# Token tiles of 32 frames from each of four batches, reads by row groups, and projections of scaled samples by weights that hold the DCT

## The chip, the cores and the metric

The kernel runs on one core of a Trainium2 chip. TensorE (PE) multiplies matrices from SBUF into PSUM, VectorE (DVE), ScalarE (ACT) and GpSimd (POOL) work on elements, SyncE (SP) issues most transfers. Each engine works through its own queue in order. The metric is the device time of one execution in microseconds: the median of three runs is 1425.93 (1425.9 to 1426.23).

## The reference, cut to what matters

64 signals of 80000 samples are cut into 157 frames of 512 samples each. Then, per signal:

```
h = frames @ D.T                                  # orthonormal DCT, 512 x 512
x = layernorm(h)
k, q = exp(i*pi*tanh(x @ Wk)), exp(i*pi*tanh(x @ Wq))   # 4 sets of 8 planes
v = x @ Wv + bv
for each set s: total += weights[s] * Re( sum over planes( cumsum(k*v) * conj(q) ) )
pos = the same with phases of the position instead of k and q
gate = sigmoid(x @ Wg + bg)
total = gate * total + (1 - gate) * sigmoid(pos_weight) * pos
h = h + x + (total / norm) @ Wo + bo              # norm = sqrt(8 * (t + 1))
x2 = layernorm(h)
scores = softmax(mean over frames(x2) @ Wg2 + bg2); e = argmax
out = h + scores[e] * (x2 @ We[e] + be[e])        # one of 16 experts per signal
```

The cumulative sum with conjugate phases is a causal attention with linear scores: (k . q) masked by j <= t, times v. All is float32.

## The kernel before, in words

The 64 signals are worked in 16 groups of four batches. A group has five tiles of 128 tokens: tile m < 4 holds the first 128 frames of batch m, and the tile `GB` (the tail) holds the last 32 frames of all four batches side by side. Samples arrive in five transfers a group (`load_frame`), already turned so that samples lie on partitions, are folded twice for the symmetries of the DCT (`fold_once`, `fold_twice`), and `embed` makes h of a tile in a PSUM pair: two matmuls of 128 columns for the even coefficients and two of 129 for cosines and sines of the odd ones, which `embed_statistics` puts together on DVE after a copy by ACT. (The first two groups use a direct table for the odd ones, L215.)

`embed_x` normalises the tile (ACT), `turn` transposes it by four TensorE transposes (L174) and a copy (L180), so that xT has features on partitions; `embed_res` keeps h + x. From xT come the phases (`project`, L519), the values (`value`, `value_product`) and the gate (`gate_product`). Values, gate and output projection use a scheme of seven half-size products for eight (`product`, L314 and L573; `token_sums`, `gather`, L317 put operands and results together), the tail tile is multiplied directly (L193).

`scores` makes the masked attention weights of a batch; `read` multiplies the values of a batch by them in full 128-row matmuls of 314 columns (157 for the content, 157 for the positions, L614) and DVE mixes the two by the gate (L604, L605). The 32-row tails are read by `read_tails` (L628), in which the four batches use four row groups of the array, into four PSUM banks; `add_tails` adds them on POOL. `output_product` adds the products into the residuals `res`, partly through u by POOL (L645). Then follow the second statistics (L161 to L168), `normal2` (ACT, L684), `turn_x2`, the routing (`route` to `pick`), an indirect fetch of the chosen expert's 1 MB per batch (`fetch`, L741), and `expert`: one matrix per batch for the tiles 0 to 3 (L193), and for the tail four matrices in four column groups of 32 (L800).

The order of the work is written out by hand: each function issues into the engines' queues in program order, and semaphores hold an instruction until its operands are ready. In group g, `project_and_values(g)` first turns x2 of group g-1, `gate(g)` follows, `experts_and_embedding(g)` runs the experts of g-1 and embeds g+1, and `attention(g)` reads and projects. PSUM is three pairs of banks in rotation (`psum`) and two single banks (`bank`). The products of the output go in the order

```
    PRODUCTS = (1, 2, 6, 5, 7, 3, 4)
```

with the second statistics of tiles 0 and 1 after product 3 and of tiles 2 and 3 after product 4. Product 1 writes r11, 2 r11, 6 r12 through u, 5 r12 and r22, 7 r21 and r22 through u, 3 r12, 4 r21 (r1 are tiles 0 and 1, r2 tiles 2 and 3, the second index the half of the columns).

Of the kernel before, what the change touches and what calls it, by code (L numbers as in the profile page):

```python
# [28 lines left out]
TL = LP - P  # L29
LT = L - P  # L30
NM = GB + 1
# [8 lines left out]
ORDER = [GB, *range(GB)]  # L40
# [3 lines left out]
def audio_tower(ctx: ExitStack, tc: tile.TileContext, a, out):  # L44

# [22 lines left out]
    small = pool("small", 6)  # L68
# [15 lines left out]
    S = [{} for _ in range(NG)]  # L84


    def load_frame(g, m):
        if g < NG:
            ft = p1.tile([P, C, P], F32, tag="frame", name="frame", bufs=NM)
            nc.sync.dma_start(out=ft, in_=a["frames"][g, m])  # L90
            S[g]["frame", m] = ft

    def fold_once(g, m):

        if g < NG:
            ft = S[g]["frame", m]
            even = p2.tile([P, 2, P], F32, tag="even", name="even")
            nc.vector.tensor_tensor(even, ft[:, :2, :], ft[:, 2:, :], ALU.add)  # L98
            nc.gpsimd.tensor_tensor(ft[:, :2, :], ft[:, :2, :], ft[:, 2:, :], ALU.subtract)
            S[g]["even", m] = even  # L100

    def fold_twice(g, m):

        if g < NG:
            ft, even = S[g]["frame", m], S[g].pop(("even", m))
            nc.vector.tensor_tensor(ft[:, 2, :], even[:, 0, :], even[:, 1, :], ALU.add)
            nc.vector.tensor_tensor(ft[:, 3, :], even[:, 0, :], even[:, 1, :], ALU.subtract)
            for n in range(2 if g > 1 else 0):
                to, by = ft[:, n, :], ft[:, 1 - n, :]
                nc.vector.scalar_tensor_tensor(to, by, lift[:, n : n + 1], to, ALU.mult, ALU.add)  # L110


    load_frame(0, 0)
    dct_e = load("dct_e", [P, 2, P])
    dct_o = p1.tile([P, 2, 2 * P], F32, tag="sum0", name="dct_o")
    nc.sync.dma_start(out=dct_o, in_=a["dct_o"])
    load_frame(0, 1)
    load_frame(0, 2)
    wv = load("wv", [P, C, D])
    load_frame(0, 3)  # L120
    load_frame(0, 4)
    lift = load("lift", [P, 2])
    trig_o = load("trig_o", [P, 2, P + 1])
    bv = load("bv", [P, D], a["bv"].partition_broadcast(P))
# [5 lines left out]
    setsel = load("setsel", [2 * F, SETS])  # L130
    hbg = load("hbg", [P, C], a["bg"])
    bo = load("bo", [P, D], a["bo"].partition_broadcast(P))
    wkq = load("wkq", [P, C, 2 * F])
    bkq = load("bkq", [P, 1])
    hmask = load("hmask", [P, L])
    hmask_t = load("hmask_t", [P, LT])
    wg = load("wg", [P, C, D])
    wo = load("wo", [P, C, D])
    rwg = load("rwg", [P, C, TL])
    rbg = load("rbg", [P, GB, E], a["rbg"].partition_broadcast(P))  # L140
    revexp = load("revexp", [P, GB, E])
    rowbase = load("rowbase", [P, 1])

    ident = const.tile([P, P], F32, name="ident", tag="ident")
    make_identity(nc, ident)
    power = const.tile([P, 1], F32, name="power", tag="power")
# [4 lines left out]
    def warm(n):  # L151

        ps = bank()
        for _ in range(n):
            nc.tensor.matmul(ps[:, :P], ident, ident, start=True, stop=True)

# [14 lines left out]
    def transposed(x):  # L171
        tr = bank()
        for c in range(C):
            nc.tensor.transpose(tr[:, c * P : (c + 1) * P], x[:, c * P : (c + 1) * P], ident)  # L174
        return tr

    def place(xT, m, tr, apart=None, copy=nc.scalar.copy):

        if m < GB:
            copy(xT[:, :, m, :P], tr.rearrange("p (c t) -> p c t", c=C))  # L180
            return
        copy(xT[:, :, :, P:], tr.rearrange("p (c b t) -> p c b t", c=C, b=GB))  # L182
        if apart is not None:
            nc.scalar.copy(apart, tr.rearrange("p (c t) -> p c t", c=C))

    def by_tail(t):

        return t.rearrange("p (b t) -> p b t", t=TL)[:, :, :LT]

    def by_tokens(ps, lhs, w):  # L190

        for c in range(C):
            nc.tensor.matmul(ps, lhs(c), w[:, c, :], start=(c == 0), stop=(c == C - 1))  # L193
        return ps


    def embed(g, m):

        s = S[g]
        if m == 0:  # L200
            s["xT"] = p1.tile([P, C, GB, LP], F32, tag="xT", name="xT", bufs=2)
            s["xT_t"] = p1.tile([P, C, P], F32, tag="xT_t", name="xT_t")
            s["res"] = []
            s["res2"] = []
        h = psum()
        h, odd = h[:, 0, :], h[:, 1, :].rearrange("p (n j) -> p n j", n=2)
        ft = s.pop(("frame", m))
        by_r = h.rearrange("p (j r) -> p r j", r=4)
        for i in range(2):
            nc.tensor.matmul(by_r[:, 2 * i, :], ft[:, 2 + i, :], dct_e[:, i, :], start=True, stop=True)  # L210
        for i in range(2):
            if g > 1:
                nc.tensor.matmul(odd[:, i, : P + 1], ft[:, i, :], trig_o[:, i, :], start=True, stop=True)  # L213
            else:
                nc.tensor.matmul(by_r[:, 1::2, :], ft[:, i, :], dct_o[:, i, :], start=(i == 0), stop=(i == 1))  # L215
        s["h", m] = h, odd

    def embed_statistics(g, m):
        s = S[g]
        h, odd = s.pop(("h", m))  # L220
        by_r = h.rearrange("p (j r) -> p r j", r=4)
        if g > 1:
# [825 lines left out]
    for m in order:  # L1048
        bias(g, m)
# [100 lines left out]
```

## Time and profile before

| what | value |
|---|---|
| median of three runs | 1425.93 us |
| the profiled execution | 1428.35 us, its span 1426.6 us |
| TensorE busy | 1414.3 us, 99% of the span, 7346 instructions |
| DVE, POOL, ACT busy | 995.0, 686.0, 493.8 us (70, 48, 35%) |
| granted TensorE clock | 0.999 |
| moved by DMA | 135.54 MB, 95 GB/s in the mean |

The span runs from the first to the last instruction of the profiled execution; its own time is 1.75 us longer. Busy time counts modelled ends of matmuls, which overlap, so for a matmul's price the start of one row of a timeline is subtracted from that of the next. A float32 matmul shows as two instructions and a transpose as one.

### The profile page before, as it was taken

What the parts mean: (1) busy time and instruction counts of PE and PEld (TensorE: products, weight loads), DVE (VectorE), ACT (ScalarE), POOL (GpSimd) and SP (SyncE); (2) the same over time, 40 slices, a digit from 0 to 9 for tenths busy, and PEclk for the clock granted to TensorE, in tenths of its full rate; (3) what the DMA queues carried; (4) which work ended last, traced back from release to release, by engine and by line L of the source; (5) the groups of instructions that cost most, each with busy time, mean ns of one, the idle gap of its engine ahead of it and who ended that gap; (6) DMA issues with size and microseconds to landing.
All of it is one profiled execution on the core that took longest, in us unless ns stands there. A gap on an engine that the chain in (4) does not pass through costs nothing.

```text
span 1426.6 us, 20573 instructions
## 1 busy us (share of the span) xinstructions
PE 1414.3 (99%) x7346; PEld 976.1 (68%) x7346; DVE 995.0 (70%) x2307; ACT 493.8 (35%) x851; POOL 686.0 (48%) x1042
## 2 busy tenths in 40 slices
PE   8999999999999999999999999999999999999998
PEld 5776676766767667676776767667676676766763
DVE  5677667676776777776777767766767677677674
ACT  4533244422434324343233442324433244422420
POOL 4454555345454453544536544455444555445432
PEclk9999999999999999999999999999999999999999
DMA  6104132051420504214042240423304142040405
GB/s 202 38 1 170 59 132 98 1 192 37 156 74 3 212 15 155 75 39 177 14 163 66 76 147 6 163 66 124 105 1 178 50 155 74 1 177 15 155 8 221
DMA packets 43157, 135.54 MB, mean 95 GB/s; under 512 B 8032, under 2 KB 8688, under 8 KB 34480
## 3 DMA queue, kind: packets, MB, share of 16 engines
q0 software_dynamic: 15616, 88.09, 16.2%
q1 hardware_dynamic: 27208, 45.90, 9.9%
q8 instruction: 59, 0.97, 0.3%
q14 instruction: 42, 0.34, 0.1%
q10 hardware_dynamic: 232, 0.24, 0.1%
HBM read 113.62 MB, written 20.58 MB: 94 GB/s over the span
## 4 chain that ended last, share of the span: by engine, by line
PE 94%; DVE 2%; DMA 2%; POOL 1%; issue 1%; another core or an unknown queue 0%; ACT 0%; SPq 0%; POOLq 0%; DVEq 0%
PE mm L314 26%; PE mm L573 15%; PE tr L193 13%; PE mm L614 10%; PE mm L193 8%; PE tr L174 5%; PE mm L800 4%; PE mm L519 2%; PE mm L210 2%; PE mm L213 2%; PE tr L700 1%; PE mm L628 1%; PE tr L590 1%; PE mm L555 1%; DMA frame<-in_frames 1%
## 5 line engine op out<-in xcount | busy, mean ns | idle before, releaser
L193 PE MATMUL tr<-we,x2T 128*128 128x512 f32 x448 | 201.4, 592 | 0.0
L165 POOL TENSOR_SCALAR rstd<-mv 128x1 f32<-128x1 f32 x160 | 39.5, 247 | 317.7 <-DVE mv L163 310.0
L614 PE MATMUL mm<-att,v 128*128 128x314 f32 x512 | 139.7, 431 | 0.0
L193 PEld LDWEIGHTS tr<-we,x2T 128*128 128x128 f32 x448 | 81.7, 190 | 82.5 <-issue 80.4
L317 DVE TENSOR_TENSOR v<-mm,v 128x512 f32<-128x512 f32 x105 | 72.3, 688 | 75.6 <-PE tr L174 50.6
L614 PEld LDWEIGHTS mm<-att,v 128*128 128x128 f32 x512 | 94.5, 189 | 38.3 <-issue 3.8
L583 ACT ACTIVATE gT<-gT,hbg 128x314 f32<-128x314 f32 x120 | 60.3, 551 | 172.4 <-DVE gT L317 166.2
L236 ACT ACTIVATE x<-mm,shift,rstd 128x512 f32<-128x512 f32 x80 | 62.2, 777 | 144.5 <-POOL shift L168 144.5
L166 POOL TENSOR_TENSOR rstd<-rstd,power 128x1 f32<-128x1 f32 x160 | 103.3, 645 | 13.3
L317 DVE TENSOR_TENSOR gT<-mm,gT 128x628 f32<-128x628 f32 x105 | 85.0, 810 | 31.3 <-PE mm L573 27.0
L174 PEld LDWEIGHTS tr<-ident,x 128*128 128x128 f32 x576 | 67.3, 141 | 51.8 <-issue 16.4
L645 POOL TENSOR_TENSOR res<-res,u 128x512 f32<-128x512 f32 x48 | 60.1, 1265 | 73.6 <-DVE u L317 73.6
L741 POOL DMA_INDIRECT we<-in_we,rows x62 | 61.6, 994 | 57.0 <-PE mm L193 40.4
L314 PE MATMUL mm<-t_o,sum 128*128 128x256 f32 x384 | 88.1, 379 | 0.0
L174 PE MATMUL tr<-ident,x 128*128 128x128 f32 x576 | 85.9, 276 | 1.2 <-DVE x2T L182 0.8
L314 PE MATMUL mm<-t_v,sum 128*128 128x256 f32 x360 | 86.7, 384 | 0.0
L317 DVE TENSOR_TENSOR res<-mm,res 128x512 f32<-128x512 f32 x96 | 64.5, 685 | 29.6 <-PE mm L314 19.0
L314 PEld LDWEIGHTS mm<-t_o,sum 128*128 128x128 f32 x384 | 73.0, 190 | 16.7 <-issue 7.7
L778 POOL DMA_INDIRECT be<-in_be,expi x75 | 71.3, 951 | 22.8 <-issue 18.6
L257 POOL TENSOR_TENSOR res<-res,bo 128x512 f32<-128x512 f32 x64 | 80.3, 1282 | 0.0
L314 PEld LDWEIGHTS mm<-t_v,sum 128*128 128x128 f32 x360 | 64.8, 190 | 10.7 <-DVE even L98 3.5
L379 POOL TENSOR_TENSOR v<-v,bv 128x1024 f32<-128x1024 f32 x30 | 70.7, 2358 | 0.0
(198 smaller groups left out, 3004.0 us busy)
## 6 DMA issues: line engine op xcount, KB each, us to landing
frame<-in_frames SPq DMA_DIRECT2D x80, 256.0 KB
out<-be SPq DMA_DIRECT2D x60, 256.0 KB
out<-be SPq DMA_DIRECT2D x60, 32.0 KB
out<-be SPq DMA_DIRECT2D x60, 26.0 KB
be<-in_be,expi POOLq DMA_INDIRECT x75
wv<-in_wv SPq DMA_DIRECT2D x1, 1024.0 KB
wg<-in_wg SPq DMA_DIRECT2D x1, 1024.0 KB
wo<-in_wo SPq DMA_DIRECT2D x1, 1024.0 KB
```

Of the source, the lines that this page charges most:

```text
L166: nc.gpsimd.tensor_tensor(rstd, rstd, power, ALU.pow)
L174: nc.tensor.transpose(tr[:, c * P : (c + 1) * P], x[:, c * P : (c + 1) * P], ident)
L193: nc.tensor.matmul(ps, lhs(c), w[:, c, :], start=(c == 0), stop=(c == C - 1))
L236: nc.scalar.activation(x, h, AF.Identity, bias=shift, scale=rstd)
L257: nc.gpsimd.tensor_tensor(r, r, bo, ALU.add)
L314: nc.tensor.matmul(ps[:, b, :], lhs[:, c, b, :P], w[:, c, :], start=(c == 0), stop=(c == 1))
L317: add = lambda to, x, y: nc.vector.tensor_tensor(to, x, y, ALU.add)
L379: nc.gpsimd.tensor_tensor(v, v, bv.unsqueeze(1).to_broadcast([P, 2, D]), ALU.add)
L573: nc.tensor.matmul(ps[:, o, : 2 * L], w[:, c, o * P : (o + 1) * P], rhs[:, c], start=(c == 0), stop=(c == 1))
L614: nc.tensor.matmul(ps[:, c, : 2 * L], s["v", i][:, cols], att[:, i], start=True, stop=True)
L741: nc.gpsimd.indirect_dma_start(out=w, out_offset=None, in_=a["we"], in_offset=bass.IndirectOffsetOnAxis(ap=s["rows"][:, b : b + 1], axis=0),)
L778: nc.gpsimd.indirect_dma_start(out=be, out_offset=None, in_=a["be"], in_offset=bass.IndirectOffsetOnAxis(ap=s["expi"][:, m : m + 1], axis=0),)
```

## The change

All five tiles of a group now have one form: tile n holds frames 32n to 32n+31 of each of the four batches, a quadrant of 32 rows per batch (`NM` = 5, tile 4 is called `TAIL`). In storage the tiles lie in the order `SLOT` (0, 1, 4, 2, 3), so that two and a half tiles make a half of 320 tokens; samples come in two transfers of halves into the buffer `xT` itself.

- **Weights with the DCT.** Wv, Wk, Wq and Wg are multiplied once, at the start, by the DCT, after their mean over the features is taken off (`through_dct`). Values, phases and gate are then computed from the folded samples, each scaled by its token's rstd. `spread` makes the scaling: rstd of a tile, broadcast, is transposed by one TensorE transpose and DVE multiplies the samples by it in place. `embed` still makes h for the residual and the statistics; `embed_x`, `turn` and their copies go.
- **Reads by quadrants.** `scores` computes, per tile and batch, 32 keys by the queries that can see them (160, 128, 96, 96 and 32 columns), four column groups side by side. `read` works a block of 128 features at a time: for each tile, four matmuls of 32 rows, one per batch, accumulate into four banks over the five tiles. `read_tails`, `add_tails` and the separate tail buffers go.
- **Experts.** Every tile holds all four batches, so every expert tile uses the four matrices in four column groups. One fetch of biases serves all tiles. The output is written in place of the residual, by four transfers a tile and eight for the last.
- **Order.** The products of values and gate go 1, 2, 6, 7, 5, 3, 4, those of the output 1, 2, 4, 6, 7, 5, 3, the output's tail comes before product 7, and the four second statistics follow the last product. The last group's weights are fetched in two parts and its experts go chunk by chunk over all tiles.
- The start is written anew for the weights; x2T has a buffer of its own; residual pairs are five instead of four.

The core of the diff (most removed lines are left out):

```diff
+Q = P // GB
+NM = LP // Q
+TAIL = NM - 1
+SLOT = [0, 1, 3, 4, 2]
+HT = P // 2
+HN = HT + 2 * P
...
+SEES = [(0, LP), (Q, LP), (2 * Q, LP), (2 * Q, LP), (2 * Q, 3 * Q)]
+START = [sum(hi - lo for lo, hi in SEES[:n]) for n in range(NM)]
+NS = sum(hi - lo for lo, hi in SEES)
...
+    def half(x, m):
+        return x[:, :, HN * m : HN * (m + 1)]
+    def tile_of(x, n):
+        return x[..., P * SLOT[n] : P * (SLOT[n] + 1)]
+    def load_half(g, m):
         if g < NG:
+            if m == 0:
+                S[g]["xT"] = p1.tile([P, C, 2 * HN], F32, tag="xT", name="xT", bufs=2)
+            nc.sync.dma_start(out=half(S[g]["xT"], m), in_=a["frames"][g, m])
...
+    def through_dct(raw, to, n):
+        ps = psum()[:, 0, :n]
+        for c in range(C):
+            nc.tensor.matmul(ps, mean, raw[:, c], start=(c == 0), stop=(c == C - 1))
+        sub(raw, raw, ps.unsqueeze(1).to_broadcast([P, C, n]))
+        yield
+        for k, parts in enumerate((((0, 1), (1, 3)), ((2, 1), (3, 3)), ((4, 0),), ((5, 2),))):
+            if k % 2 == 0:
+                ps = psum()
+            for i, (table, r) in enumerate(parts):
+                nc.tensor.matmul(
+                    ps[:, k % 2, :n], tables[:, table], raw[:, r], start=(i == 0), stop=(i == len(parts) - 1)
+                )
+            if k % 2:
+                nc.scalar.copy(to[:, k - 1 : k + 1], ps[:, :, :n])
+                yield
...
+        sines = p2.tile([P, P + 1], F32, tag="sines", name="sines")
+        nc.scalar.copy(sines, odd[:, 1, : P + 1])
+        add(by_r[:, 1, :], odd[:, 0, :P], sines[:, :P])
+        sub(by_r[:, 3, :], odd[:, 0, 1 : P + 1], sines[:, 1 : P + 1])
         rstd, shift = statistics(h)
         rstd1 = small.tile([P, 1], F32, tag="rstd1", name="rstd1")
         nc.gpsimd.tensor_scalar(rstd1, rstd, 1.0, None, ALU.add)
...
+    def embed_res(g, n):
+        s = S[g]
+        h, shift, rstd1 = s.pop(("st", n))
+        if n == TAIL:
             r = p1.tile([P, D], F32, tag="res_t", name="res_t", bufs=2)
         else:
+            if n % 2 == 0:
+                s["res2"].append(p1.tile([P, 2, D], F32, tag="res", name="res", bufs=5))
+            r = s["res2"][-1][:, n % 2, :]
         nc.scalar.activation(r, h, AF.Identity, bias=shift, scale=rstd1)
...
+    def spread(g, n):
+        s = S[g]
+        tr = bank()[:, :P]
+        nc.tensor.transpose(tr, s["rstd", n].to_broadcast([P, P]), ident)
+        x = tile_of(s["xT"], n)
+        nc.vector.tensor_tensor(x, x, tr.unsqueeze(1).to_broadcast([P, C, P]), ALU.mult)
...
+    def alike(first, second):
+        n = 2 * P
+        yield first[:, :, :n], second[:, :, -n:]
+        if first.shape[2] > n:
+            yield first[:, :, n:], second[:, :, :-n]
+    def token_sums(g, x, tail=True):
+        S[g]["blocks"] = blocks = halves(x)
+        n = HN if tail else 2 * P
+        (a11, a12), (a21, a22) = [[y[:, :, :n] for y in blocks[0]], [y[:, :, -n:] for y in blocks[1]]]
+        S[g]["sums"] = made = [
+            p1.tile([P, 2, HN], F32, tag=f"sum{i}", name="sum")[:, :, :n] for i in range(4)
+        ]
+        for (to, x), (_, y) in zip(alike(made[0], a21), alike(made[0], a22)):
+            add(to, x, y)
+        yield
+        sub(made[1], made[0], a11)
+        yield
+        for (to, y), (x, _) in zip(alike(made[2], a21), alike(a11, a21)):
+            sub(to, x, y)
+        yield
+        sub(made[3], a12, made[1])
...
+    def gather(i, ps, c):
         (c11, c12), (c21, c22) = c
         if i == 1:
+            nc.scalar.copy(c12, ps)
         elif i == 2:
+            add(c11, ps, c12)
+        elif i == 7:
+            for (x, to), (y, _) in zip(alike(ps, c21), alike(c12, c21)):
+                add(to, x, y)
+        elif i == 5:
+            add(c12, ps, c12)
+            for (x, to), (_, y) in zip(alike(ps, c22), alike(ps, c21)):
+                add(to, x, y)
+        elif i == 4:
             add(c21, ps, c21)
+        else:
             add(c12, ps, c12)
...
+    def scores(g):
         ps = bank()
+        for n in range(NM):
+            lo, hi = SEES[n]
             for i in range(GB):
+                to = ps[Q * i : Q * (i + 1), START[n] : START[n] + hi - lo]
+                nc.tensor.matmul(to, kf[:, SLOT[n], i], qf[:, lo // Q : hi // Q, i], start=True, stop=True)
+        nc.vector.tensor_tensor(att[:, 0], ps[:, :NS], hmask, ALU.mult)
+        nc.vector.tensor_tensor(att[:, 1], att[:, 0], share, ALU.add)
...
+    def read(g, c):
+        s = S[g]
+        if c % 2 == 0:
+            parts = [psum(), psum()]
+        else:
+            parts = [psum(), bank().unsqueeze(1), bank().unsqueeze(1)]
+        banks = [ps[:, b, : 2 * LP] for ps in parts for b in range(ps.shape[1])]
+        for n in range(NM):
+            for i in range(GB):
+                q = slice(Q * i, Q * (i + 1))
+                lo, hi = SEES[n]
+                to = banks[i].rearrange("p (s t) -> p s t", s=2)[:, :, lo:hi]
+                by = att[q, :, START[n] : START[n] + hi - lo]
+                nc.tensor.matmul(
+                    to, s["v", n][q, c * P : (c + 1) * P], by, start=(n == 0), stop=(n == TAIL)
+                )
+        i = 0
+        for ps in parts:
+            of = slice(i, i + ps.shape[1])
+            i = of.stop
+            r = ps[:, :, : 2 * LP].rearrange("p b (s n t) -> p b s n t", s=2, n=NM)
+            th = s["gT"][:, c].rearrange("p (n b t) -> p b n t", n=NM, b=GB)[:, of]
+            for n, op in enumerate((ALU.mult, ALU.add)):
+                nc.vector.tensor_tensor(th, r[:, :, n], th, op)
...
+    def fetch(g, rooms=(), parts=1):
+        s = S[g]
+        ws = [
+            rooms[b] if b < len(rooms) else p1.tile([P, C * D], F32, tag="we", name="we", bufs=GB) for b in range(GB)
+        ]
+        n = C * D // parts
+        of = a["we"].rearrange("r (k n) -> (r k) n", k=parts)
+        for k in range(parts):
+            rows = t("rows", [P, GB], I32)
+            base = rowbase[:, parts + k - 1 : parts + k]
+            nc.vector.tensor_scalar(rows, s["rev"], float(-P * parts), base, ALU.mult, ALU.add)
+            for b in range(GB):
+                nc.gpsimd.indirect_dma_start(
+                    out=ws[b][:, n * k : n * (k + 1)],
+                    out_offset=None,
+                    in_=of,
+                    in_offset=bass.IndirectOffsetOnAxis(ap=rows[:, b : b + 1], axis=0),
+                )
+        s["ws"] = [w.rearrange("p (c o) -> p c o", c=C) for w in ws]
...
+    def add_bias(g, n):
+        s = S[g]
+        nc.vector.scalar_tensor_tensor(s["res"][n], s["be"], s["gate"], s["res"][n], ALU.mult, ALU.add)
+    def expert_chunk(g, n, c, ps):
+        s = S[g]
+        for i in range(GB):
+            nc.tensor.matmul(
+                ps[Q * i : Q * (i + 1), :],
+                s["x2T"][:, c, i, Q * n : Q * (n + 1)],
+                s["ws"][i][:, c, :],
+                start=(c == 0),
+                stop=(c == C - 1),
+            )
+    def expert_out(g, n, ps):
+        s = S[g]
+        o = s["res"][n]
+        nc.vector.scalar_tensor_tensor(o, ps, s["gate"], o, ALU.mult, ALU.add)
+        for i in range(GB):
+            for lo, hi in ((0, Q),) if n < TAIL else ((0, Q // 2), (Q // 2, LT)):
+                queue = nc.sync if g + 1 < NG or i % 2 == 0 else nc.scalar
+                queue.dma_start(out=out[GB * g + i, Q * n + lo : Q * n + hi, :], in_=o[Q * i + lo : Q * i + hi, :])
+    def expert(g, n, between=lambda c: None):
+        ps = bank() if g + 2 < NG else psum()[:, 0, :]
+        for c in range(C):
+            between(c)
+            expert_chunk(g, n, c, ps)
+        expert_out(g, n, ps)
...
     def project_and_values(g):
         keep_product(g)
-        fold_once(g + 1, 1)
         route(g - 1)
         route_sum(g - 1)
-        value_product(g, 7)
+        value_product(g, 5)
         keep_product(g)
         route_spread(g - 1)
         pick(g - 1)
-        fetch(g - 1, range(GB))
-        value(g, GB)
+        fetch(g - 1)
+        value(g, TAIL)
         weigh()
         pick_gate(g - 1)
-        keep_value(g, GB)
+        keep_value(g, TAIL)
         value_product(g, 3)
+        keep_product(g)
+        value_product(g, 4)
         fold_twice(g + 1, 0)
         keep_product(g)
-        value_product(g, 4)
-        fold_twice(g + 1, 1)
-        keep_product(g)
...
     def gate(g):
-        for m in range(NM):
-            bias(g - 1, order[m])
-        fold_once(g + 1, 2)
-        fold_once(g + 1, 3)
+        bias(g - 1)
+        fold_once(g + 1, 1)
         for n, i in enumerate(PRODUCTS):
             gate_product(g, i)
-            if n == 0:
-                scores(0)
-            elif n == 1:
-                scores(2)
-                scores_of_tails()
-            elif n in (4, 5):
-                fold_twice(g + 1, n - 2)
+            if n == 1:
+                scores(g)
+            elif n == 4:
+                fold_twice(g + 1, 1)
...
     def experts_and_embedding(g):
         new = g + 1
+        add_bias(g - 1, TAIL)
+        expert(g - 1, TAIL)
+        embed(new, 0)
+        embed_statistics(new, 0)
+        embed_res(new, 0)
         add_bias(g - 1, 0)
+        load_half(g + 2, 0)
+        load_half(g + 2, 1)
+        expert(g - 1, 0)
+        embed(new, 1)
+        spread(new, 0)
+        embed_statistics(new, 1)
+        embed_res(new, 1)
         add_bias(g - 1, 1)
+        add_bv(g, 0)
+        expert(g - 1, 1)
+        embed(new, 2)
+        spread(new, 1)
+        embed_statistics(new, 2)
+        embed_res(new, 2)
         add_bias(g - 1, 2)
         add_bv(g, 1)
         expert(g - 1, 2)
         embed(new, 3)
+        embed(new, TAIL)
+        spread(new, 2)
         embed_statistics(new, 3)
+        embed_statistics(new, TAIL)
+        embed_res(new, 3)
+        embed_res(new, TAIL)
+        add_bias(g - 1, 3)
         expert(g - 1, 3)
...
     def attention(g):
...
+        for c in range(C):
+            read(g, c)
+        made = token_sums(g, S[g]["gT"], tail=False)
+        next(made)
+        next(made)
         if g == 0:
+            for n in range(NM):
+                add_bo(1, n)
+        for i in (1, 2, 4, 6, 7, 5, 3):
+            if i == 7:
+                output_tail(g)
+                statistics2(g, TAIL)
+                normal2(g, TAIL)
+            output_product(g, i)
+            if i in (2, 4):
                 next(made)
+            if ahead:
+                if i == 1 and g > 0:
+                    spread(g + 1, 3)
+                elif i == 5:
+                    spread(g + 1, TAIL)
+        for n in range(TAIL):
+            statistics2(g, n)
...
+    fetch(g, [w.rearrange("p c o -> p (c o)") for w in (wv, wg)], parts=2)
     pick_gate(g)
...
+    bias(g)
+    for n in (3, 4):
+        add_bias(g - 1, ORDER[n])
+        expert(g - 1, ORDER[n])
+    banks = [ps[:, k, :] for ps in [psum() for _ in range(3)] for k in range(2)]
+    for c in range(C):
+        for n in range(NM):
+            if c == 0:
+                add_bias(g, n)
+            expert_chunk(g, n, c, banks[n])
+            if c == C - 1:
+                expert_out(g, n, banks[n])
```

## The prediction

> **What bounds the kernel now.** I read the page's first part and its chain, then TensorE's timeline of one steady group, then the other engines over the same stretch.
>
> ```profile
> PE 1414.3 (99%) x7346; PEld 976.1 (68%) x7346; DVE 995.0 (70%) x2307; ACT 493.8 (35%) x851; POOL 686.0 (48%) x1042
> PE 94%; DVE 2%; DMA 2%; POOL 1%; issue 1%; another core or an unknown queue 0%; ACT 0%; SPq 0%; POOLq 0%; DVEq 0%
> ```
>
> TensorE is busy for 99% and carries 94% of the chain: a removed matmul pays in full only while the others still deliver in time. Timeline of TensorE (start, us, engine, line, tiles, count), around the reads and after the output products:
>
> ```profile
> 592.52 1.11 PE L628 MATMUL mm<-att_t,v_t 32*128 32x58 f32 x32
> 593.57 8.72 PE L614 MATMUL mm<-att,v 128*128 128x314 f32 x32
> 602.13 3.62 PE L314 MATMUL mm<-wo,gT 128*128 128x256 f32 x16
> ...
> 617.65 0.60 PE L174 MATMUL tr<-ident,x_t 128*128 128x128 f32 x4
> 618.18 2.33 PE L519 MATMUL mm<-xT,wkq 128*64 128x314 f32 x16
> 620.44 0.66 PE L174 MATMUL tr<-ident,x 128*128 128x128 f32 x4
> 620.94 1.89 PE L314 MATMUL mm<-wv,xT 128*128 128x256 f32 x8
> ```
>
> The start of one row to the next gives the true pitch, the modelled ends overlap. A matmul is two instructions, a transpose one. Pitches per instruction: 128 columns 0.111 us, 256 0.216, 314 0.265, 512 0.429, a transpose 0.109. Reads start at 506.27, 593.64, 681.01 in the chain: 87.37 us a group, and the rows leave no gap in it.
>
> The others over the same stretch (DVE, POOL, ACT timelines):
>
> ```profile
> 595.16 0.48 DVE L604 TENSOR_TENSOR gT<-mm,gT 128x314 f32<-128x314 f32 x1
> 595.67 0.49 DVE L605 TENSOR_TENSOR gT<-mm,gT 128x314 f32<-128x314 f32 x1
> ...
> 616.12 0.69 DVE L317 TENSOR_TENSOR res<-mm,res 128x512 f32<-128x512 f32 x1 [1.03 <-PE mm L314]
> 616.85 0.69 DVE L161 BATCH_NORM_STATS2 st<-res 128x6 f32<-128x512 f32 x1
> ```
>
> ```profile
> 615.17 2.49 POOL L645 TENSOR_TENSOR res<-res,u 128x512 f32<-128x512 f32 x2 [1.28 <-DVE u L317]
> 617.85 0.22 POOL L165 TENSOR_SCALAR rstd<-mv 128x1 f32<-128x1 f32 x1 [0.19 <-DVE mv L163]
> 618.15 0.57 POOL L166 TENSOR_TENSOR rstd<-rstd,power 128x1 f32<-128x1 f32 x1
> 618.82 0.27 POOL L168 TENSOR_SCALAR shift<-mv,rstd 128x1 f32<-128x1 f32 x1
> ```
>
> ```profile
> 619.12 0.82 ACT L684 ACTIVATE x<-res,shift,rstd 128x512 f32<-128x512 f32 x1 [0.25 <-POOL shift L168]
> ```
>
> This is the chain from residual to normalised tile 0: add at 616.12, turned at 620.44, 4.3 us. It costs nothing today, since product 4 (1.73), the tail's turn and `project` run on TensorE meanwhile.
>
> **What the Trainium skill says.** "TensorE: Matmul & The Clock Gate", Measured speedup vs the span model: four row groups (K=32) of 512 columns ran 3.07 times as fast as one after another. The trace agrees in kind: L628 does eight rounds of four in 1.05 us, 131 ns each, where four in a row of 58 columns would need 4 x 58 x 0.84 = 195. "TensorEngine Tiling (Array Packing)", Key Properties: a switch of tiling mode drains the engine. Agrees: the transposes beside L519 take 0.53 and 0.50 against 0.44, some 0.1 us at each edge. Same page, PSUM Bottleneck: after a fourfold matmul speedup the copies out of PSUM may bind. Today they don't; below they do.
>
> **The change, part by part.** The sum is against the profiled execution, 1428.35 us with a span of 1426.6; the median is 1425.93, so I add the difference to the median.
>
> *TensorE alone, no waits.* (1) Turning x goes: 20 transposes a group become 5 of rstd, -15 x 0.109 = -1.64, in the 14 groups embedded in steady state: -23. (2) Reads: today 9.7 (592.52 to 602.13 and an edge). After: per column block five rounds of 320, 256, 192, 192, 64 columns, twice: 2 x (0.267 + 0.213 + 0.160 + 0.160 + 0.112) = 1.82 if four overlap fully (the last as weight loads allow in L628), four times and two edges 7.5: -2.2 x 16 = -35. At 3.07 instead of 4: 27.3 us of single streaming / 3.07 = 8.9, hence -0.8; with no overlap beyond the two that L628 proves, 13.7, +4. I take 7.5: L800's column groups overlap fully (32 instructions in 3.57 us are 0.446 a round of four). (3) Experts: 4 x 3.43 + 3.77 = 17.5 becomes 5 x (3.43 + 0.2 edges) = 18.15: +0.66 x 15 = +10. (4) 320 columns for 314: 64 slots x 5 ns = +0.32 x 15 = +5. (5) Scores 1.46 to 1.35: -1.5. Sum -45.
>
> *DVE, ACT, POOL, DMA traffic.* ACT loses ten 0.6-0.8 us passes a group; POOL loses the tail adds (4 x 0.50) and four bias fetches (0.95 each); DVE gains five `spread` multiplications (0.65 each). These queues have room as totals. All four expert matrices are now wanted at the first expert tile: the fetch at 636.1 has landed by about 650 (400 GB/s there), and the fetch still precedes the experts by 3.4 + 3.5 + 16.5 = 23 us; hidden, unless landing slows by 9 us. SP issues 24 output transfers a group instead of 12, 0.34 us each, 8 of 85 us; the loads of samples, ahead of them, have their buffer once the gate ends. Hidden by a whole attention stage. The residuals get five pairs of buffers, so `embed_res` of tile 2 needs the old tile 1's output written: issued some 2 us before, at worst a microsecond of ACT, which is 35% busy; if that cover is gone it lengthens wait C. The gate's gathering is split in two more pieces, at 2.1 us of TensorE a product against 0.8 to 1.8 of DVE: hidden.
>
> *New wait A, after the output products (15 times).* The order is now 1, 2, 4, 6, 7, 5, 3, and all four second statistics follow product 3. Let product 3 end at 0 on TensorE. Product 7 ended at -3.5; its u add ends at -2.7. POOL has the tail's rstd until -2.15, then two adds of 1.25: until 0.4. Product 5's add into tiles 2 and 3 must wait for that (before, 5 preceded 7): DVE 0.5 to 1.15; the last `spread`, queued behind it, to 1.8. `project`, ready at 0.5, reads the scaled samples: starts at 1.9, 1.4 late, ends at 4.2. Product 3's add runs 1.8 to 2.45, statistics to 3.35, POOL 1.26 to 4.65, ACT 0.8 to 5.5, turn at 5.6: another 1.4. Sum 2.8 x 15 = +42. Even with POOL and DVE free, 0.2 + 0.65 + 0.9 + 1.3 + 0.9 + 0.1 = 4.1 against a cover of 2.9 leaves 1.2 (+18). Queued behind the turn on TensorE are all value products.
>
> *New wait B, in the reads (16 times).* Per block DVE takes 4 operations of 320 elements at 0.48, or 2 and 4 of 160 at 0.34: 8.4 us for four blocks. From the end of block 0, product 2 (which needs blocks 2 and 3) can start after 0.2 + 8.4 + 0.1 = 8.7; TensorE has three blocks, product 1 and a spread, 7.5. Wait 1.2 x 16 = +20 (8.0 us of DVE: +12). Behind it wait all later output products, and on DVE the token sums come after the gating, so no slack is regained before the tail's 3.4 us.
>
> *New wait C, before the reads (14 times).* Block 0 needs the PSUM pair of embed 3. DVE holds `spread` 2 until embed 4 is through, then embed 3's statistics (1.6), POOL four steps (1.4), ACT (0.8), in all 0.2 + 0.65 + 1.6 + 0.1 + 1.4 + 0.8 + 0.1 = 4.85 after `spread` 2; cover is one expert tile 3.65; all reads are queued behind, and wait B counts from their block 0, so the two add. Wait 1.1 x 14 = +15 (0.6: +8).
>
> Waits: 77, at least 38.
>
> *Start.* Reads of group 0 begin at 68.3 today. After, TensorE waits for samples, tables and raw wv, 2.1 MB, about 9.0 at the traced rates of the first 10 us, then for a 2048-element DVE subtraction and copies (3.2); its work is 8.6 (wv) + 2.2 (wkq) + 8.6 (wg) through the DCT, 17.2 values, 8.9 ten embeds, 17.3 gate, 2.5 project, 1.3 + 1.3 share and scores, 1 spreads: 69. Sum 81-82, +14 (10 to 19).
>
> *End.* The turns come 1.9 later (wait A's tail), edges 0.8. The old weights are read until the last old expert tile, so the second two of four fetches wait 7.2 us more; six issues at 1.25, landing 2 later, give the first half at +11.6 of the fetch and TensorE then has 20 chunks of 0.86: ends near 29, today 25.5. +6 (3 to 9).
>
> Sum: -45 + 77 + 14 + 6 = +52: 1478.
>
> **The rivals.** *TensorE stays without gaps:* the waits are covered. For it: no gap in 87 us today. Against: the queues above are in-order and the cover is counted. Then -45 + 20 = -25: 1401. It decides faster or slower at a wait of 1.7 us a group ((45 - 20) / 15). *Half the waits* (38): +13, 1439. *Row groups overlap little:* twice only, reads take 13.7, +6.2 x 16 less wait B's 20: +79, 1557; against it L628's rate. *Weights or samples late:* 2 us a group of DMA wait, +30: 1508; against it 9 us of room.
>
> **How the numbers follow.** Forecast's waits in full 0.62 (own range 1455 to 1500), half 0.17, row groups or DMA 0.08, gapless 0.13. Of the half case 0.03 falls to no change or faster. Within 0.2% (2.9 us, about what this kernel's measurement can tell) 0.03; faster 0.13; slower 0.84. The range reaches from half the waits with the small start, 1432, to the DMA case, 1508.
>
> **What would show it.** A: `project` waiting for DVE and the first turn of x2 waiting for ACT, some 2.8 us a group, with the residual add of product 5 released by POOL. B: product 2 released by DVE's gating. C: a read released by ACT's `embed_res`. Step 2: about 1.8 us per block of reads. Group period near 89.5. A period under 86 makes me wrong; so does a gapless TensorE.

## The result, and the profile after

The changed kernel takes 1510.39 us (1506.47 to 1510.91) against 1426.07 for the kernel before: 1.0585 times as long, interval 1.0567 to 1.0604. The prediction was 1478 with a range to 1508. The sign was right, the size 32 us short.

The profiled execution has a span of 1508.3 us, 81.7 more than before's 1426.6. Cut at the first read of group 0 and the first read of group 15:

| stretch | before | after | difference | predicted |
|---|---|---|---|---|
| start, to the first read of group 0 | 68.25 | 101.1 | +32.9 | +14 |
| middle, 15 groups | 1287.9 | 1321.5 | +33.7 | +32 |
| end, from the first read of group 15 | 70.5 | 85.6 | +15.2 | +6 |
| one steady group | 87.37 | 89.44 | +2.07 | near 89.5 |

The middle came as forecast in sum; nearly all of the miss lies in the start (19) and the end (9). The page's busy line of TensorE and its chain by engine:

```profile
PE 1434.1 (95%) x10646; PEld 941.6 (62%) x10646; DVE 1003.3 (67%) x2150; ACT 398.2 (26%) x691; POOL 606.0 (40%) x849
PE 80%; DVE 8%; POOL 6%; ACT 3%; issue 2%; DMA 1%; SPq 0%; POOLq 0%; DVEq 0%
```

TensorE held 94% of the chain before. DVE, POOL and ACT now hold 17% instead of 3%: stretches in which TensorE waits for a chain of small operations. The waits of TensorE by line and releaser (us in total, times, longest):

```profile
PE tr L661 <- ACT x L648: 21.1, 17, 1.4
PE mm L501 <- DVE xT L281: 16.5, 15, 1.2
PE mm L193 <- DMA wv<-in_wv: 5.4, 1, 5.4
PE mm L591 <- ACT res L268: 3.8, 14, 0.3
PE mm L763 <- DMA we<-in_we,rows: 3.4, 1, 3.4
```

The first two are wait A, 1.1 and 1.3 us in each of 15 groups; the fourth marks wait C. The list puts only 0.27 us a group on C, because the modelled ends of the matmuls ahead of it reach into the wait; the starts show it whole. TensorE's rows in one group's reads: block 0 starts, stops and goes on, blocks 1, 2 and 3 start, and product 1 follows:

```profile
641.12 0.81 PE L591 MATMUL mm<-att,v 32*128 32x320 f32 x4
642.20 1.40 PE L591 MATMUL mm<-att,v 32*128 32x320 f32 x22 [0.27 <-ACT res L268]
...
644.07 0.54 PE L591 MATMUL mm<-att,v 32*128 32x320 f32 x2
...
645.97 1.99 PE L591 MATMUL mm<-att,v 32*128 32x320 f32 x29
...
648.12 0.48 PE L591 MATMUL tr<-att,v 32*128 32x320 f32 x1
...
650.47 1.99 PE L349 MATMUL mm<-wo,gT 128*128 128x256 f32 x8
```

The first four instructions of block 0 start at 641.12 and the next 1.08 us later, behind ACT's residual. Selected rows at the end of the same group's output products show A link by link:

```profile
663.02 0.69 DVE L97 TENSOR_TENSOR u<-mm,u 128x512 f32<-128x512 f32 x1 [0.16 <-PE mm L349]
664.14 2.50 POOL L608 TENSOR_TENSOR res<-res,u 128x512 f32<-128x512 f32 x2
...
666.67 0.69 DVE L97 TENSOR_TENSOR res<-mm,res 128x512 f32<-128x512 f32 x1 [1.30 <-POOL res L608]
667.28 0.68 DVE L281 TENSOR_TENSOR xT<-xT,tr 128x512 f32<-128x512 f32 x1
...
668.01 2.37 PE L501 MATMUL mm<-xT,wkq 128*64 128x320 f32 x16 [1.09 <-DVE xT L281]
...
671.73 0.66 PE L661 MATMUL tr<-ident,x 128*128 128x128 f32 x4 [1.34 <-ACT x L648]
```

Product 7's sum on DVE, two adds on POOL, product 5's add held for them, the spread behind it, and only then `project`; the turn of tile 0 follows another 1.34 late. Before, the same operations ran while TensorE had product 4, the tail's turn and `project`.

### The profile page after: what moved, and what is told of

It reads as the page before. It is cut to its first block, busy times and chain, and to the rows that moved or that the text cites. A ratio compares the mean times of both kernels' runs of the same rounds, so it can differ in the third digit from the quotient of the medians.

```text
span 1508.3 us, 26805 instructions
## 1 busy us (share of the span) xinstructions
PE 1434.1 (95%) x10646; PEld 941.6 (62%) x10646; DVE 1003.3 (67%) x2150; ACT 398.2 (26%) x691; POOL 606.0 (40%) x849
## 4 chain that ended last, share of the span: by engine, by line
PE 80%; DVE 8%; POOL 6%; ACT 3%; issue 2%; DMA 1%; SPq 0%; POOLq 0%; DVEq 0%
PE mm L349 20%; PE mm L554 15%; PE tr L763 13%; PE mm L224 8%; PE mm L591 7%; DVE st L211 3%; PE mm L239 3%; POOL res L608 3%; PE mm L763 2%; PE mm L241 2%; PE tr L661 2%; PE tr L591 2%; POOL rstd L216 2%; DVE xT L281 1%; PE tr L671 1%
## 5 line engine op out<-in xcount | busy, mean ns | idle before, releaser
L763 PE MATMUL tr<-we,x2T 128*32 128x512 f32 x2240 | 254.8, 595 | 0.0
L763 PEld LDWEIGHTS tr<-we,x2T 128*32 128x32 f32 x2240 | 65.6, 109 | 140.8 <-issue 139.1
L97 DVE TENSOR_TENSOR gT<-mm,gT 128x128 f32<-128x128 f32 (+1 forms) x135 | 87.0, 673 | 89.6 <-PE mm L554 88.1
L591 PE MATMUL mm<-att,v 32*128 32x192 f32 (+2 forms) x1536 | 136.1, 378 | 5.9 <-ACT res L268 3.8
L591 PEld LDWEIGHTS mm<-att,v 32*128 32x128 f32 x1536 | 102.5, 186 | 29.8 <-issue 12.5
L601 DVE TENSOR_TENSOR gT<-mm,gT 128x320 f32<-128x320 f32 x192 | 91.1, 489 | 32.0 <-PE mm L591 20.6
L564 ACT ACTIVATE gT<-gT,hbg 128x320 f32<-128x320 f32 x120 | 59.6, 554 | 169.0 <-DVE gT L97 169.0
L281 DVE TENSOR_TENSOR xT<-xT,tr 128x512 f32<-128x512 f32 x80 | 54.7, 684 | 38.1 <-PE tr L279 38.0
L648 ACT ACTIVATE x<-res,shift,rstd 128x512 f32<-128x512 f32 x64 | 52.1, 815 | 98.2 <-POOL shift L218 74.9
L224 PE MATMUL mm<-wv,xT 128*128 128x512 f32 x160 | 74.7, 611 | 2.2 <-DVE v L398 2.0
```

Of the source, the lines that this page charges most:

```text
L97: add = lambda *x: nc.vector.tensor_tensor(*x, ALU.add)
L224: nc.tensor.matmul(ps, tile_of(x[:, c], n), w[:, c, :], start=(c == 0), stop=(c == C - 1))
L281: nc.vector.tensor_tensor(x, x, tr.unsqueeze(1).to_broadcast([P, C, P]), ALU.mult)
L591: nc.tensor.matmul(to, s["v", n][q, c * P : (c + 1) * P], by, start=(n == 0), stop=(n == TAIL))
L601: nc.vector.tensor_tensor(th, r[:, :, n], th, op)
L763: nc.tensor.matmul(ps[Q * i : Q * (i + 1), :], s["x2T"][:, c, i, Q * n : Q * (n + 1)], s["ws"][i][:, c, :], start=(c == 0), stop=(c == C - 1),
```

## The experiments

Differences are given against the changed kernel: the difference of the two ratios to the kernel before, times 1426 us. Two intervals of about 0.18% make each uncertain by some 3.6 us.

**Wait A alone.**

```
-        for i in (1, 2, 4, 6, 7, 5, 3):
+        for i in (1, 2, 6, 5, 7, 3, 4):
...
+            if i == 3:
+                statistics2(g, 0)
+                statistics2(g, 1)
```

> The changed kernel with its output products back in the order 1, 2, 6, 5, 7, 3, 4 (tail before 5, sums, spreads and second statistics placed to suit: those of tiles 0 and 1 ahead of product 4). If wait A is the chain that the prediction named (product 7's two adds on POOL, then product 5's add, the last spread and project; then product 3's add, statistics and the first turn of x2), the 1.09 + 1.34 us a group vanish: -2.4 x 15 = -37, 1474 us, group period 87.0. If TensorE's work or another queue sets the period and these waits only stand where they do, they move elsewhere: -10 or less, 1500 or more.

Ratio 1.0288 (1.0273 to 1.0304), -42 us. A steady group takes 86.91 us, 2.53 less, 38 us over 15 groups; both waits are gone from the list of TensorE's waits. In this kernel's timeline product 4 stands ahead of the turns, and no row carries a wait:

```profile
645.83 1.89 PE L349 MATMUL mm<-t_o,gT 128*128 128x256 f32 x8
647.56 0.60 PE L661 MATMUL tr<-ident,x_t 128*128 128x128 f32 x4
648.09 2.37 PE L501 MATMUL mm<-xT,wkq 128*64 128x320 f32 x16
650.40 0.66 PE L661 MATMUL tr<-ident,x 128*128 128x128 f32 x4
```

The order of the products is half of the whole loss. With it restored a group is 0.46 us shorter than before the change.

**Wait C alone.**

```
+        embed_statistics(new, 3)
         spread(new, 2)
-        embed_statistics(new, 3)
```

> The changed kernel with embed 3's statistics ahead of spread 2 on DVE, nothing else. If wait C is DVE's order (statistics held back by a spread that waits for embed 4), block 0 of the reads no longer waits for ACT's residual: -1.1 x 14 = -15, 1495 us, with wait B unchanged at 0.95 a group. If wait B or the release of the tail's residual takes its place: -5 or less, 1505 or more.

1.0527 (1.0512 to 1.0543), -8 us; a group is 0.59 shorter instead of 1.1. Tile 3's residual no longer stops the reads, but in its place stands the tail's, whose PSUM pair block 1 needs (TensorE's waits of this kernel; the 2.1 is the one in group 0):

```profile
PE mm L591 <- ACT res_t L268: 6.2, 15, 2.1
```

**Wait B alone.** The gating without its addition:

```
-            for n, op in enumerate((ALU.mult, ALU.add)):
+            for n, op in enumerate((ALU.mult,)):
```

> The changed kernel with the addition of the read's second half left out of the gating (one DVE operation per part instead of two), so the gated values lack that term. If wait B is DVE's gating, 8.4 us for 7.5 of TensorE, it is gone: -0.95 x 16 = -15, 1495 us, and wait C stays. If the reads are long for TensorE's own work (edges between row groups), no change beyond -3.

1.0471 (1.0454 to 1.0488), -16 us; a group is 0.72 shorter (11 us in 15 groups; the other 5 are not to be seen in its profiled run, whose start and end differ from the changed kernel's by +2.5 and -2.4). The reads take 8.64 us instead of 9.35, and product 2 follows product 1 at the same distance in both kernels (1.94). Where the reads became shorter is seen from the starts of the four column blocks; the same rows of this kernel:

```profile
639.54 0.81 PE L591 MATMUL mm<-att,v 32*128 32x320 f32 x4
...
642.49 0.54 PE L591 MATMUL mm<-att,v 32*128 32x320 f32 x2
...
644.38 1.85 PE L591 MATMUL mm<-att,v 32*128 32x320 f32 x32
...
646.23 0.49 PE L591 MATMUL mm<-att,v 32*128 32x320 f32 x2
...
648.18 1.99 PE L349 MATMUL mm<-wo,gT 128*128 128x256 f32 x8
```

From start to start, with the experiment before and one that follows (us):

| kernel | block 0 | block 1 | block 2 | block 3 | reads |
|---|---|---|---|---|---|
| changed | 2.95 | 1.90 | 2.15 | 2.35 | 9.35 |
| C alone: statistics first | 2.36 | 1.89 | 1.84 | 2.66 | 8.75 |
| B alone: half the gating | 2.95 | 1.89 | 1.85 | 1.95 | 8.64 |
| cover, second arrangement | 1.90 | 1.97 | 2.70 | 2.27 | 8.84 |

DVE does pace the reads, but the wait, 0.7 us, is inside them, in blocks 2 and 3, and not ahead of product 2, where the prediction put it. By the code, these blocks write the PSUM that blocks 0 and 1 used; in the changed kernel DVE's last gating of block 1 runs just as block 3 is to begin:

```profile
647.11 1.26 DVE L601 TENSOR_TENSOR gT<-tr,gT 128x160 f32<-128x160 f32 x4
```

The table also separates the two waits. C is the surplus of block 0, 1.05 us. With C's cause removed, blocks 2 and 3 take 4.50 us together, as before; with B's removed, block 0 takes 2.95, as before. Neither shrinks the other; what C's removal didn't bring is the tail's residual, which leaves block 0 at 2.36. No run removed both.

**Cover for B and C.** Embeds one expert tile earlier, the last expert tile between the reads and product 1, a sixth pair of residuals:

```
         for c in range(C):
             read(g, c)
+        if ahead and g > 0:
+            expert(g - 1, 3, ps=psum()[:, 0, :])
```

> The changed kernel with the embeds one expert tile earlier (0 and 1 ahead of expert tile 0, 2 and 3 ahead of tile 1, the tail ahead of tile 2), six pairs of residuals, and the last expert tile behind the reads, as cover for the gating. If B and C are waits without cover and nothing else, both vanish in 14 groups: -(0.95 + 1.1) x 14 = -29, 1481 us. If DVE's total, or a later buffer, takes their place: -15 or less, 1495 or more.

1.1170 (1.1152 to 1.1187), +83 us: worse than any other. Most groups took 95.6 us; expert tiles waited for the output add of an earlier tile in DVE's queue, up to 4.1 us at a time, and reads for POOL's add of the bias of the values. The likely reason, argued and not isolated, is ACT's order: each pair's second copy of sines stood behind the first's residual, which waits for POOL. The second arrangement copies both sines first, and also places the embeds anew:

> As the kernel with the last expert tile behind the reads, but the embeds placed so that both copies of a pair's sines stand ahead of its residuals on ACT, with 0 and 1 ahead of expert tile 0, the tail and 2 ahead of tile 1, and 3 ahead of tile 2, so that no embed's chain of DVE, POOL and ACT is shorter of cover than 4.0 us. If the first arrangement failed only by the order of the three queues: B and C vanish, -29, 1481 us. If the move of expert tile 3 itself costs (PSUM, rows of DVE): 1495 or more.

1.0567 (1.0550 to 1.0584), -3 us, no difference that can be told; 89.43 us a group. C is gone, and the time is the same. The stretch of one group's reads in this kernel (us, then busy time of TensorE, weight loads, DVE, ACT, POOL):

```profile
639.52:648.36 8.84, 8.73 (x161) 7.80 (x160) 8.46 (x18) 0.78 (x1) 7.51 (x8) 1.00 0.12 32
```

DVE is busy for 8.46 of 8.84 us. Ahead of its first gating stood a bias add, an output add, a spread and one more bias add, which took 1.65 us where the others take 0.72. POOL's adds of `bo` had begun just before it; whether they slowed it was not isolated:

```profile
640.50 4.17 POOL L273 TENSOR_TENSOR res<-res,bo 128x512 f32<-128x512 f32 x3
...
640.67 1.65 DVE L757 SCALAR_TENSOR_TENSOR res<-be,gate,res 128x512 f32<-128x512 f32 x1
```

So the gating began 0.8 us after the end of block 0 instead of 0.1. The cover stood behind the reads, where the prediction had seen B; inside the reads B grew, and blocks 1 to 3 took 0.54 us more. A new 0.47 us wait of expert tile 3 for DVE came on top. Together that is nearly the 1.05 us of C: the arrangement exchanged C for a longer B and a new wait.

**The start without the weights' transform.** `load("wv", ...)` straight into place, likewise `wkq` and `wg`, and all steps of `through_dct` out.

> The changed kernel with wv, wkq and wg loaded into their places as they are: their mean and their products with the DCT's tables are left out, 19.4 us of TensorE's work by the prediction's count, so the values, gates and scores are those of other weights. If the start is late by TensorE's work alone, it shrinks by 19 to 20: 1490 us, first read of group 0 near 81. If the transform also brought the waits for DVE's subtraction and ACT's copies and the low clock after them (some 12 us), 1476 to 1482, first read near 69.

1.0442 (1.0426 to 1.0458), -20 us. The first theory: the transform costs what its matmuls cost, 19.4 predicted. Yet the first read comes at 84.2, 17 earlier than with the transform and still 16 later than before the change, without any of the transform's work. The other loss is elsewhere.

**The clock in the start.** Two of the rows of the changed kernel's start, and its windows (us, TensorE and the other engines busy, then the granted clock):

```profile
11.00 5.27 PE L193 MATMUL mm<-wv,mean 128*128 128x512 f32 x8 [5.44 <-DMA wv<-in_wv]
...
36.50 6.16 PE L224 MATMUL mm<-wv,xT 128*128 128x512 f32 x8
```

```profile
28.00:32.00 4.00, 3.07 (x14) 1.63 (x13) 0.64 (x3) 0.94 (x2) 1.13 (x4) 1.00 0.01 2
32.00:36.00 4.00, 2.67 (x18) 2.29 (x18) 1.82 (x4) 0.93 (x2) 1.21 (x4) 0.84 0.01 4
36.00:40.00 4.00, 4.00 (x8) 1.96 (x8) 1.48 (x4) 0.43 (x2) 0.93 (x3) 0.50 0.00 0
40.00:44.00 4.00, 4.00 (x9) 1.81 (x8) 0.75 (x1) 0.78 (x1) 0.28 (x2) 0.81 0.00 0
```

Eight instructions of 512 columns take 5.3 and 6.2 us where 3.6 is the usual in this kernel. So idle products were added, first in rough sizes (`warm(n)` issues n of them):

> The changed kernel with 128-column products of the identity, read by nothing, put where TensorE waits in the start (24 more ahead of the weights' mean, 18 after it, 3, 4, 8, 16 in the first values, 8 and 16 in the first gate). They add work and remove none. If the idle time lowers the clock, and this is what the start lost beside its work, the mean's 5.27 becomes 3.4 and the 6.8 us lost at 0.50 to 0.84 of the clock come back: -6 to -10, 1500 to 1504 us, granted clock 1.00 up to the reads. If the clock falls for another reason: 0 to +4.

1.0572 (1.0558 to 1.0587), -2 us: undecided. The clock was 1.00 in nearly all of the start and the mean took 3.60, but a product of 128 columns costs 0.22 us, so 18 after the mean were 1.5 us too many, and 16 stood ahead of a tile that did not wait. Sized to the waits:

> The changed kernel with products that nothing reads in the start once more, now sized to the waits that they stand in (0.22 us each: 24 more ahead of the weights' mean, 10 after it, 2, 3 and 5 in the first values, 9 ahead of the fourth value tile, 5 and 8 in the first gate). If idle time lowers the clock: granted clock 1.00 up to the reads, the mean in 3.4 instead of 5.3, no product at half speed, -6 to -9: 1501 to 1504 us. If a fuller TensorE gains no time, since the waits after it only grow: -2 to +2.

1.0523 (1.0508 to 1.0537), -9 us, by adding work. The mean granted clock was 0.995 to 0.998 in its five runs, against 0.988 to 0.992 in the four of the changed kernel. The same stretches of that kernel:

```profile
10.60 3.67 PE L193 MATMUL mm<-wv,mean 128*128 128x512 f32 x8
...
34.08 3.65 PE L224 MATMUL mm<-wv,xT 128*128 128x512 f32 x8
```

```profile
36.00:40.00 4.00, 4.00 (x11) 1.76 (x10) 1.05 (x3) 0.78 (x1) 1.21 (x4) 1.00 0.00 0
```

The first read comes at 95.6 instead of 101.1. The kernels that share the start code agree: counted from 24 us to the reads, the clock lost 6.8 us (4 us times what each window lacked to 1.00) in the changed kernel and five others, and the first read came at 101.1 to 104.0; in the run of the first experiment it lost 1.7, and the read came at 97.8. That run also shows that the idle time alone doesn't decide. Its matmuls between 28 and 36 us are those of the changed kernel, its longest wait is 0.98 us as there, its TensorE was no busier, and its clock stayed at 1.00:

```profile
28.00:32.00 4.00, 3.07 (x14) 1.59 (x12) 0.53 (x2) 0.94 (x2) 1.24 (x4) 1.00 0.07 15
32.00:36.00 4.00, 2.48 (x18) 2.15 (x19) 1.93 (x5) 0.93 (x2) 1.21 (x4) 1.00 0.02 4
36.00:40.00 4.00, 4.00 (x13) 2.00 (x13) 1.49 (x5) 0.44 (x3) 1.21 (x4) 1.00 0.00 0
```

Why the clock fell in one run and not in the other stays open.

**The end.** Rows of the last fetch computed in the routing; four rooms that nobody reads any more:

```
+    rooms = [wv, wg, t_v, t_o]
...
+        if g == NG - 1:
+            s["rows"] = [rows_of(g, 2, k) for k in range(2)]
...
-    fetch(g, [w.rearrange("p c o -> p (c o)") for w in (wv, wg)], parts=2)
...
+    fetch(g, flat, parts=2)
```

> The changed kernel with the last group's expert rows computed in its routing, ahead of the old expert tile's output add on DVE, and with wv, wg and the two sets of weight sums as rooms for all four matrices, so that no fetch waits for old weights. If the end is late for rows (1.9 us) and for the rooms (4.0 us), the fetches start 5.9 us earlier, the 8.4 us wait of TensorE shrinks to about 2.5 and less of the last tiles runs at a low clock: -6 to -10, 1500 to 1504 us. If the transfers themselves set the end: -2 or less.

1.0536 (1.0521 to 1.0551), -7 us; in its profiled run, one of the longer ones, the end is 3.3 us shorter and the start 2.1 longer. In the changed kernel the fetches began at 1468.03, the third waited until 1473.41 for old weights, and the last was issued at 1479.61. TensorE in that time, and at the last tiles:

```profile
1475.45 1.05 PE L763 MATMUL mm<-wg,x2T_last 128*32 128x512 f32 x2 [1.20 <-DMA wg<-in_we,rows]
1479.91 2.79 PE L763 MATMUL mm<-we,x2T_last 128*32 128x512 f32 x3 [3.41 <-DMA we<-in_we,rows]
...
1498.24 0.62 PE L763 MATMUL mm<-wv,x2T_last 128*32 128x512 f32 x1 [0.84 <-DVE res L774]
1501.04 0.62 PE L763 MATMUL mm<-wv,x2T_last 128*32 128x512 f32 x1 [0.87 <-DVE res L774]
```

With the repair all eight issues followed one another without a wait for old weights, and TensorE's idle times ahead of new weights, for which its profile names no releaser, shrank to 0.4, 0.8 and 0.8. The last two rows are waits for DVE's output add. The likely cause, from the code, is that two tiles have the two banks of one PSUM pair, so that the next tile waits while DVE reads the other; the sum of repairs takes the banks from different pairs, and these two waits are gone there.

**All repairs together.**

> All repairs in one: products in the order 1, 2, 6, 5, 7, 3, 4 (-42 measured), embed 3 one expert tile earlier (C, -15), rooms and rows for the last fetch (-6) and its tiles' banks taken from different PSUM pairs (-1.7), in the start two embeds and idle products where TensorE waits (-9), the first gate's spreads one tile later and its tail's embed two tiles earlier (-5). If they add: 1510 - 79 = 1431 us. If they hide one another: 1440 or more.

1.0159 (1.0145 to 1.0174): 1451 us beside 1428 for the kernel before, 1449 on the scale of the forecast, not 1431. The end took 75.3 us (85.6 before the repairs, of which A's order is 2.9) and kept its clock at 1.00, and a group 86.63. The start did not add: first read at 98.7. The spread moved out of the way only uncovered the product behind it, which waited 4.17 us for ACT's residual, itself behind ACT's sines and DVE's folds, and the clock fell again.

> The same repairs, with the last expert tile behind the reads and the embeds as in that experiment, in place of the shift of embed 3 alone. If wait B goes too: 1431 - 14 = 1417 us, faster than the kernel before by 10. If the move costs what the first arrangement cost: 1500 or more.

1.0170 (1.0155 to 1.0184): the same again, so the cover behind the reads bought nothing here either.

> The first sum of repairs, with two more: spread 2 after output product 6 (its use of a single bank made expert tile 3 wait 0.6 to 1.1 for tile 2's output add in 14 groups), and in the start embeds 0 and 1 of group 1 with their statistics ahead of ACT's sines of group 0, 2 and 3 ahead of the third gate part, the tail ahead of the fourth (the 4.17 and 3.47 us for ACT's residuals, and the low clock after them). If they add: -9 and -10 from 1451: 1432 us, within 0.5% of the kernel before. If the waits move to the next product once more: 1445 or more.

1.0140 (1.0123 to 1.0157), 1449 us beside 1428. The start gained 5.5 (first read at 93.3), the groups nothing: 86.76 us, and expert tile 3's wait, once gone, came back one stage on, in the reads:

```profile
PE mm L591 <- ACT res_t L267: 10.2, 15, 0.7
```

So no version that was run beats the kernel before. Its groups are 0.6 to 0.7 us shorter than before, some 10 us in all, against 25 us of a longer start and 6 of a longer end.

## Why the prediction was right and wrong

- *Wait A* was right in place, chain and size: 2.8 us a group forecast, 2.53 measured by its removal. Of the rivals, a gapless TensorE (1401) is far off, and so is little overlap of the row groups: the reads take 9.35 us with their waits, not 13.7. Late weights or samples are not seen either: no wait of the steady groups is put down to a DMA.
- *Wait B* (1.2 us a group, 20 in all, forecast) came out at 0.7 and 11, and its place was wrong: blocks 2 and 3 of the reads, not product 2. *Wait C* (1.1 forecast, though its own terms, 4.85 less 3.65, give 1.2) is 1.05, right in place, chain and size; its removal brought 0.59, since the tail's residual stood behind it. "So the two add" is not refuted: neither changed when the other was removed.
- *TensorE alone*, -45, was too good. A group became 2.07 longer with waits of 2.53, 0.7 and 1.05, so the work saved is 2.2 us, where the prediction's terms give 3.0. By stages, the kernel before against the one with A's order restored: expert tiles and embeds 24.22 to 23.43 us, output products, to which spreads have moved, 15.52 to 15.96, reads 9.61 to 7.59 without B and C, the rest +0.15. The reads kept 2.0 of their 2.2; experts, embeds and output products together saved 0.35, where steps (1) and (3) make 1.0. The middle's good fit thus is luck in part: work 0.8 a group too good and waits 0.8 too long cancel.
- *Start*, +14, is the step that failed most: +33. Its sum of TensorE's work is roughly borne out (the transform, 19.4 forecast; without it the first read came 17 earlier and the run was 20 shorter, waits included). It took every matmul at full clock and counted no wait behind the first weights' transform. By the trace: weights at 11.0 instead of 9.0, +2.0; the mean, +1.8; low clock up to the reads, 6.8; eight further waits of 0.2 to 2.0 each, 7.7. Sum 18.3 of the 19 missing. The sized idle products recovered 5.5 of them by the first read (9, uncertain by 3.6, by the ratio); moving embeds and spreads recovered some 2 more. The rest is read from the trace and was not removed.
- *End*, +6, is +15. The wait for old weights was in the sum. Missing were the rows queued behind an old tile's output add on DVE (1.9 us), the low clock after TensorE's wait (the windows from 1476 to 1488 lack 3.4 us, part of it while TensorE still waited), and the two waits for DVE at the last tiles (1.7): up to 7 of 9. Rooms, rows and pairs together, in the sum of repairs, shortened the end by 7.4.
- The sign held since both sides of the sum that decided it, A and the steady period, were right. The range was too narrow at the top because it varied the waits in the groups and left start and end at 9 and 6 us of width.

## What to carry to other kernels

Price the start and the end with their waits and their clock, not by their work: where TensorE is fed in small pieces a short wait can be paid twice, once as a gap and once as slow matmuls behind it. Before an order of products is changed, follow the last sum through every queue to the next stage's first matmul; here that order cost as much as everything else. And before a wait is covered, find its place by the starts of the matmuls, and look at what the cover puts into the queue that releases it: here an expert tile stood behind the reads while the wait was inside them, and a bias add ahead of the gating, slower than the others, held it back.

## What the runs showed of the hardware

The clock can fall on less idleness than expected. The Trainium skill, "TensorE: Matmul & The Clock Gate", Why this matters for your kernels, says that idle gaps of over about 3 us between bursts bring TensorE back to half speed. The end agrees: 0.50 in the window after waits of 1.2 and 3.41 us. The start goes beyond that sentence: no wait between 28 and 36 us was longer than 0.98, TensorE was busy for 3.07 and 2.67 of each 4 us, and the clock fell to 0.50 in the window after. With idle products in those gaps it was 1.00; but in the first experiment's run it was 1.00 too, without them (3.07 and 2.48). The mean's eight matmul instructions took 5.27 us for 3.6 in windows whose recorded clock was 1.00, so the duration of a known matmul is the better witness.

Four row groups overlapped more fully than the 3.07 times that the prediction quotes from the same page: in an undisturbed block (block 1, 644.07 to 645.97) one round of four follows another after 0.27 us at 320 columns, 0.21 at 256 and 0.16 at 192, the pitches of a single stream that the prediction assumed for full overlap. The whole block took 1.90 us. A quarter of the prediction's 27.3 us of single streaming is 6.8, so by this estimate the block, with its slower first and last rounds, is 3.6 times as fast as its matmuls one after another.
